# Second self-attention: where sums, inverses, scaling and output products stand in the slots

## Chip, cores and metric

The kernel runs on one core of one Trainium2 chip. The metric is the time of one execution on the device in microseconds (us), lower is better; the median of several runs is compared.

## What is computed

Two transformer blocks run one after the other over x of shape (8, 512, 256): eight batch rows ("batches" here) of 512 tokens. All arithmetic is float32. The change is in the first attention of the second block, self-attention with 16 heads of width 64 and rotary positions:

```
attn_in = adaln(x, cond)
q, k, v = attn_in @ wq, attn_in @ wk, attn_in @ wv      # (512, 1024) each, 16 heads of 64
q, k = rope(q), rope(k)
a = softmax(q @ k.T * 64 ** -0.5)                       # per head, 512 x 512
x = (a @ v) @ wo + bo + x                               # heads joined, 1024 -> 256
```

Softmax is computed without subtracting a maximum: the exponentials are multiplied with v first, and the result is divided by the exponentials' sums afterwards.

## The kernel before

The kernel runs through phases: the first block (to about 835 us), this self-attention (about 835 to 1820 us), and cross-attention with the feed-forward part (to the end). In every phase the order of the work on TensorE (PE), VectorE (DVE), ScalarE (ACT) and GpSimd (POOL) is the order in which the Python code issues it: the block is under a manual schedule, and nothing is reordered. Each engine runs its own instructions in that order and waits for data and buffers. DMAs of this phase are issued from SyncE's queue (SP), also in order.

**Blocks and groups.** A batch's 16 heads are four groups `g` of four heads; keys are four tiles `kt` of 128. A block is one pair (g, kt): `score(g, kt)` makes 8 products into two tiles ps_S (each two PSUM banks), which ACT turns with two exponentials (L1020) into two tiles p (six buffers in all). `value(g, kt)` multiplies p with v into the banks ps_O and ps_D, over the four kt; after the last one ACT copies them into two tiles oT (L1043).

**Sums of a group.** At kt 0 POOL adds the p tiles of kt 0 and 1 into two tiles sm (L1035). At kt 2 DVE adds those of kt 2 and 3 (four operations L1039). Then `sums(g)` adds over the 128 partitions by products with ones (`ones32`, 32 columns wide) into a bank ps_X; ACT copies it to den (L1055), and two DMAs bring it through DRAM into a tile rec. `inverse(g)` is a reciprocal (L1067) and two small reductions (L153) on DVE, a DMA to DRAM (rec_d) and four DMAs that spread it over partitions into two tiles rb. `scaled(g)` multiplies both oT with rb on POOL (L1085). When all eight oT of a batch are scaled, `out_tiles(0)` and `out_tiles(1)` multiply them with w_so, 32 products each into one ps_X bank, and DVE adds the bank to x (L464).

**Preparing q, k, v.** `values(half, ts)` computes two token tiles of v into two ps_X banks, which ACT copies (L989). `queries(g)` and `keys(g)` make two banks each; DVE multiplies each bank with cosines (L999) and sines (L1000) into four tiles t, and POOL combines them (L1002, L1003). There are two ps_X banks, used in turn by values, queries, keys, sums, outputs and the transposes of `turn`.

**Slots.** A slot m holds two blocks: scores of block 2m+1, then the jobs of that slot, then scores of block 2m+2, then values of blocks 2m and 2m+1, then what `after` holds. A batch b has eight slots, `base = 8 b`; this text counts them 0 to 7. Even slots compute values of kt 0 and 1, odd ones of kt 2 and 3. The jobs of batches in the middle, in order (next: of the batch after; prev: of the batch before):

| slot | jobs between the two scores | after the values |
|---|---|---|
| 0 | values, sums(3, prev), keys(1), layer-norm statistics (next) | inverse(3, prev) |
| 1 | values, queries(2), scaled(3, prev) | |
| 2 | output 0 (prev), sums(0), keys(2), statistics (next) | layer-norm rows (next), inverse(0) |
| 3 | output 1 (prev), queries(3), row addition to x (POOL, L448), scaled(0) | |
| 4 | keys(3), sums(1), turn (next): 8 transposes (L427) | inverse(1) |
| 5 | queries(0, next), scaled(1) | |
| 6 | values (next), sums(2), keys(0, next) | inverse(2) |
| 7 | values (next), queries(1, next), scaled(2) | |

The place of sums comes from `mid`, which is put behind the slot's first job. In the first batch, slot 4 has a memset as its first job, so sums stand ahead of the keys there.

Of the kernel before, what the change touches and what calls it, by code (L numbers as in the profile page):

```python
# [17 lines left out]
B, N, D, H, T, CD, FF = 8, 512, 256, 16, 64, 192, 1024  # L18
# [67 lines left out]
def fast_path(ctx: ExitStack, tc: tile.TileContext, a: dict, out: bass.AP):  # L86
# [878 lines left out]
    with tc.tile_pool(name="ph4", bufs=2) as wk:  # L965
        NG = H // 4
        kb, vb = kv_first()
        first_rows = []
        steps, mid, after = {}, {}, {}

        def last(slot, fn):
            steps.setdefault(slot, []).append(fn)
# [152 lines left out]
        for b, (score, value, sums, inverse, scaled, out_tiles, _) in enumerate(todo):  # L1125
            base = 2 * NG * b
            for g in range(NG):
                if b == B - 1 and g == NG - 1:
                    break
                n = base + 2 * g + 2  # L1130
                mid[n] = lambda g=g, f=sums: f(g)
                after.setdefault(n, []).append(lambda g=g, f=inverse: f(g))
                last(n + 1, lambda g=g, f=scaled: f(g))
            if b < B - 1:
                for qp in range(2):
                    steps[base + 2 * NG + 2 + qp].insert(0, lambda qp=qp, f=out_tiles: f(qp))

        def slots():
            n = B * NG * NT
# [1029 lines left out]
@with_exitstack  # L2169
def tile_kernel(ctx: ExitStack, tc: tile.TileContext, a: dict, out: bass.AP):  # L2170
    nc = tc.nc
    with ExitStack() as fast:
        good = fast_path(fast, tc, a, out)
        flag = nc.values_load(good[0:1, 0:1], min_val=0, max_val=1,
                              skip_runtime_bounds_check_because="it is made by a comparison")
    with tc.If(flag == 0):
        with ExitStack() as general:
            general_path(general, tc, a, out)
# [86 lines left out]
```

## Time and profile before

| | us |
|---|---|
| median of 3 runs (lowest, highest) | 2419.1 (2417.03, 2423.43) |
| the profiled execution's own time | 2413.91 |
| its span, first to last instruction | 2411.8 |
| one batch in the middle of this self-attention | 122.5 |

| engine | busy us | share of the span |
|---|---|---|
| PE (products) | 2379.0 | 99% |
| DVE | 1139.5 | 47% |
| POOL | 966.5 | 40% |
| ACT | 889.2 | 37% |

The granted TensorE clock is 0.998 of full speed. A line of the timeline gives the start (us from the span's start), the time to the end of the last merged instruction, the engine, the line of the kernel, what is written and read, how many instructions are merged and, in brackets, how long the engine was idle before them and what released it. Every product in float32 shows as two instructions. Products are pipelined, so their ends overlap the next start: differences of starts are the better measure.

### The profile page before, as it was taken

How to read it: one execution, taken by the hardware profiler on the slowest of the kernel's cores; microseconds unless marked ns; L12 is line 12 of the kernel's file. 1: busy time of each engine (PE TensorE's matmuls, PEld its weight loads, DVE VectorE, ACT ScalarE, POOL GpSimd, SP SyncE). 2: the span in 40 equal slices, each digit the busy share in tenths (PEclk: the TensorE clock that was granted, in tenths of full speed). 3: DMA queues.
4: the chain of work that ended last, by engine and by line, in shares of the span. 5: the costliest groups of instructions: out<-in, count | busy, mean ns of one | idle time of the engine just before them, and what ended most of it. 6: DMA issues, size and time to landing. Idle time of an engine off the chain costs nothing.

```text
span 2411.8 us, 28553 instructions
## 1 busy us (share of the span) xinstructions
PE 2379.0 (99%) x10964; PEld 1158.8 (48%) x10964; DVE 1139.5 (47%) x2115; ACT 889.2 (37%) x1118; POOL 966.5 (40%) x588
## 2 busy tenths in 40 slices
PE   9999999999999999999999999999999999999998
PEld 4333544544545633434343444444445556567665
DVE  4564534434345344555454555545445656651110
ACT  4665545545442134333333333333342212221221
POOL 4563323323201046555555554646453445441110
PEclk9999999999999999999999999999999999999999
DMA  5130000000002001000101010100023212210000
GB/s 184 33 107 11 16 15 13 16 14 6 12 11 92 0 1 32 14 24 10 28 10 28 10 28 10 28 10 26 30 67 95 77 58 68 64 56 31 18 22 20
DMA packets 84897, 84.07 MB, mean 35 GB/s; under 512 B 42656, under 2 KB 59792, under 8 KB 84752
## 3 DMA queue, kind: packets, MB, share of 16 engines
q1 hardware_dynamic: 83208, 78.99, 11.0%
q8 instruction: 88, 1.44, 0.2%
q0 software_dynamic: 640, 2.10, 0.2%
q10 hardware_dynamic: 904, 1.07, 0.2%
q14 instruction: 57, 0.47, 0.1%
HBM read 72.09 MB, written 10.04 MB: 34 GB/s over the span
## 4 chain that ended last, share of the span: by engine, by line
PE 87%; DVE 4%; POOL 3%; issue 3%; DMA 1%; ACT 1%; SPq 1%; POOLq 0%; DVEq 0%; ACTq 0%
PE ps_X L116 36%; PE ps_S L116 22%; PE ps_D L116 13%; PE ps_O L116 13%; PE ps_X L427 1%; DMA rb<-rec 1%; DVE t L843 1%; POOL x L448 1%; DVE sm L1039 1%; POOL p L1277 1%; ACT p L590 0%; PE ps_X L610 0%; POOL var L561 0%; DVE t L1000 0%; SPq L1270 0%
## 5 line engine op out<-in xcount | busy, mean ns | idle before, releaser
L116 PE MATMUL ps_S<-q,k 32*128 32x512 f32 (+1 forms) x3072 | 425.6, 623 | 5.5 <-ACT p L590 3.4
L1020 ACT ACTIVATE p<-ps_S 128x1024 f32<-128x1024 f32 x256 | 250.8, 1022 | 459.7 <-PE ps_S L116 450.3
L590 ACT ACTIVATE p<-ps_S 128x1024 f32<-128x1024 f32 x256 | 248.3, 1022 | 171.6 <-PE ps_S L116 170.3
L116 PEld LDWEIGHTS ps_S<-q,k 32*128 32x128 f32 (+1 forms) x3072 | 148.7, 183 | 244.8 <-issue 155.5
L1039 DVE TENSOR_TENSOR sm<-sm,p 128x1024 f32<-128x1024 f32 x128 | 252.1, 2028 | 0.1
L999 DVE TENSOR_TENSOR t<-ps_X,rope_c 128x512 f32<-128x512 f32 x126 | 87.0, 690 | 341.0 <-PE ps_X L116 341.0
L1002 POOL TENSOR_TENSOR q<-t 128x512 f32<-128x512 f32 x32 | 65.5, 2047 | 294.3 <-DVE t L1000 294.3
L182 POOL TENSOR_TENSOR rstd<-rstd,mhalf 128x4 f32<-128x4 f32 x49 | 51.2, 1044 | 293.6 <-DVE rstd L181 292.6
L844 POOL TENSOR_TENSOR q<-t,t 128x512 f32<-128x512 f32 x72 | 94.9, 1319 | 172.6 <-DVE t L843 171.6
L116 PE MATMUL ps_X<-hT,w 128*128 128x512 f32 x328 | 151.0, 597 | 0.5 <-DVE t L780 0.5
L1035 POOL TENSOR_TENSOR sm<-p 128x1024 f32<-128x1024 f32 x64 | 149.7, 2364 | 1.9 <-ACT p L1020 1.9
L1085 POOL TENSOR_TENSOR oT<-oT,rb 128x512 f32<-128x512 f32 x63 | 128.9, 2065 | 19.6 <-DMA rb<-rec_d 19.6
L116 PE MATMUL ps_O<-p,v 128*64 128x512 f32 x512 | 134.9, 605 | 0.0
L116 PE MATMUL ps_D<-p,v 128*64 128x512 f32 x512 | 131.6, 592 | 0.0
L116 PE MATMUL ps_O<-p,h 128*32 128x512 f32 x1024 | 129.5, 609 | 0.6 <-ACT p L590 0.6
L621 POOL TENSOR_TENSOR attn<-attn,gate 128x256 f32<-128x256 f32 x32 | 23.3, 727 | 250.7 <-DVE attn L619 250.7
L116 PE MATMUL ps_X<-w_sa_wv,hT 128*128 128x512 f32 x256 | 118.0, 604 | 0.0
L1002 POOL TENSOR_TENSOR k<-t 128x512 f32<-128x512 f32 x32 | 40.7, 1272 | 192.8 <-DVE t L1000 192.8
L116 PE MATMUL ps_X<-hT,w_sa_wq 128*128 128x512 f32 x256 | 115.9, 595 | 0.0
L116 PE MATMUL ps_X<-w_sa_wo,oT 128*128 128x256 f32 x512 | 114.5, 382 | 0.1
L116 PE MATMUL ps_X<-hT,w_sa_wk 128*128 128x512 f32 x248 | 114.6, 605 | 0.0
L116 PE MATMUL ps_S<-hT,w_ff_w 128*128 128x512 f32 x256 | 111.3, 593 | 0.0
(286 smaller groups left out, 3663.6 us busy)
## 6 DMA issues: line engine op xcount, KB each, us to landing
rb<-rec SPq DMA_DIRECT2D x128, 128.0 KB
rb<-rec_d SPq DMA_DIRECT2D x124, 128.0 KB
rb<-rec SPq DMA_DIRECT2D x16, 256.0 KB
out_dram<-x SPq DMA_DIRECT2D x15, 256.0 KB
x<-in_x_dram SPq DMA_DIRECT2D x7, 512.0 KB
gate<-modd SPq DMA_DIRECT2D x24, 128.0 KB
k_d<-q POOLq DMA_DIRECT2D x8, 256.0 KB, 2.4
v_d<-v SPq DMA_DIRECT2D x8, 256.0 KB
```

What stands on the lines that cost most here:

```text
L116: nc.tensor.matmul(o, lhsT, rhs, start=start, stop=stop)
L182: nc.gpsimd.tensor_tensor(r[:, :n], r[:, :n], mhalf[:, :n], ALU.pow)
L427: nc.tensor.transpose(ps[:, t * P : (t + 1) * P], z[:, t, k * P : (k + 1) * P], ident)
L448: nc.gpsimd.tensor_tensor(xs[b], xs[b], r[:, None, :].to_broadcast([P, NT, D]), ALU.add)
L590: nc.scalar.activation(pr[u], pss[u], AF.Exp, scale=HD0 ** -0.5)
L844: nc.gpsimd.tensor_tensor(dst, t1, t2, ALU.add)
L999: nc.vector.tensor_tensor(c, ps, rope_c, ALU.mult)
L1002: nc.gpsimd.tensor_tensor(r[0], ec, os, ALU.subtract)
L1020: nc.scalar.activation(pr, pss[u], AF.Exp, scale=HD1 ** -0.5)
L1035: nc.gpsimd.tensor_tensor(sm, s["p", g, 0, u], s["p", g, 1, u], ALU.add)
L1039: nc.vector.tensor_tensor(s["sm", g, u], s["sm", g, u], s["p", g, t, u], ALU.add)
L1085: eng.tensor_tensor(o, o, s["rb", g, u], ALU.mult)
```

## The change

For the groups of every batch but the last, sums move from between the slot's jobs to the head of what follows the slot's values; the inverse moves from the end of that slot to the end of the next slot's jobs; scaling moves one slot further. Both output products of a batch stand together at the head of slot 3 of the next batch, instead of one in slot 2 and one in slot 3. The groups of the last batch keep their places.

```diff
                 n = base + 2 * g + 2
-                mid[n] = lambda g=g, f=sums: f(g)
-                after.setdefault(n, []).append(lambda g=g, f=inverse: f(g))
-                last(n + 1, lambda g=g, f=scaled: f(g))
+                if b == B - 1:
+                    mid[n] = lambda g=g, f=sums: f(g)
+                    after.setdefault(n, []).append(lambda g=g, f=inverse: f(g))
+                else:
+                    after.setdefault(n, []).insert(0, lambda g=g, f=sums: f(g))
+                    last(n + 1, lambda g=g, f=inverse: f(g))
+                last(n + 1 + (b < B - 1), lambda g=g, f=scaled: f(g))
             if b < B - 1:
-                for qp in range(2):
-                    steps[base + 2 * NG + 2 + qp].insert(0, lambda qp=qp, f=out_tiles: f(qp))
+                steps[base + 2 * NG + 3][0:0] = [lambda qp=qp, f=out_tiles: f(qp) for qp in range(2)]
```

The slots of a batch in the middle after the change:

| slot | jobs between the two scores | after the values |
|---|---|---|
| 0 | values, keys(1), statistics (next), scaled(2, prev) | sums(3, prev) |
| 1 | values, queries(2), inverse(3, prev) | |
| 2 | keys(2), statistics (next), scaled(3, prev) | sums(0), layer-norm rows (next) |
| 3 | output 0, output 1 (prev), queries(3), row addition to x, inverse(0) | |
| 4 | keys(3), turn (next), scaled(0) | sums(1) |
| 5 | queries(0, next), inverse(1) | |
| 6 | values (next), keys(0, next), scaled(1) | sums(2) |
| 7 | values (next), queries(1, next), inverse(2) | |

## Prediction

> **What bounds the kernel now.** I read the page first, then PE's timeline over one batch of the second self-attention (122.5 us a batch), then the timelines of POOL, ACT and DVE beside it, and the waits.
>
> ```profile
> PE 2379.0 (99%) x10964; PEld 1158.8 (48%) x10964; DVE 1139.5 (47%) x2115; ACT 889.2 (37%) x1118; POOL 966.5 (40%) x588
> ```
>
> PE is the bound: 99% busy. In one batch of this phase (1181.40 to 1303.90) it is busy 122.00 of 122.50 us, so the change is worth what it does to PE's own sequence, and what new waits it puts before PE. PE's timeline, slots 0 and 1, then slot 4 (start, us, ...):
>
> ```profile
> 1211.58 2.00 PE L116 MATMUL ps_S<-q,k 32*128 32x512 f32 x16
> 1213.51 3.70 PE L116 MATMUL ps_X<-w_sa_wv,hT 128*128 128x512 f32 x8
> 1217.14 1.06 PE L116 MATMUL ps_X<-sm,ones 128*32 128x512 f32 x8
> 1218.14 3.70 PE L116 MATMUL ps_X<-hT,w_sa_wk 128*128 128x512 f32 x8
> 1221.77 2.00 PE L116 MATMUL ps_S<-q,k 32*128 32x512 f32 x16
> ...
> 1227.28 2.00 PE L116 MATMUL ps_S<-q,k 32*128 32x512 f32 x16
> 1229.21 3.70 PE L116 MATMUL ps_X<-w_sa_wv,hT 128*128 128x512 f32 x8
> 1232.75 3.60 PE L116 MATMUL ps_X<-hT,w_sa_wq 128*128 128x512 f32 x8
> ...
> 1280.87 3.70 PE L116 MATMUL ps_X<-hT,w_sa_wk 128*128 128x512 f32 x8
> 1284.94 1.06 PE L116 MATMUL ps_X<-sm,ones 128*32 128x512 f32 x8 [0.37 <-DVE t L1000]
> 1286.14 1.23 PE L427 MATMUL ps_X<-ident,z 128*128 128x128 f32 x8
> 1287.30 2.00 PE L116 MATMUL ps_S<-q,k 32*128 32x512 f32 x16
> ```
>
> The reader is to see starts, not durations: start to start, values, sums, keys take 8.26 (1213.51 to 1221.77), values and queries without sums 7.07 (1229.21 to 1236.28). So sums in the middle cost 1.20. The only wait is slot 4's 0.37. Sums that stand behind values already exist at the end of the phase (PE's timeline again):
>
> ```profile
> 1791.75 1.03 PE L116 MATMUL ps_D<-p,v 128*64 128x512 f32 x4
> 1792.70 1.07 PE L116 MATMUL ps_X<-sm,ones 128*32 128x512 f32 x8
> 1793.70 2.00 PE L116 MATMUL ps_S<-q,k 32*128 32x512 f32 x16
> ```
>
> Values to sums 0.95, sums to scores 1.00; elsewhere values to scores take 0.96. So sums there cost 0.99.
>
> POOL of slot 0, and a scaling pair with nothing in its way; ACT of slot 1; and one line of ACT's waits over seven batches (us, times, longest):
>
> ```profile
> 1223.38 1.27 POOL L1002 TENSOR_TENSOR k<-t 128x512 f32<-128x512 f32 x1 [6.94 <-DVE t L1000]
> 1225.84 4.67 POOL L1035 TENSOR_TENSOR sm<-p 128x1024 f32<-128x1024 f32 x2
> ...
> 1787.58 2.56 POOL L1085 TENSOR_TENSOR oT<-oT,rb 128x512 f32<-128x512 f32 x2 [4.30 <-DMA rb<-rec_d]
> ```
> ```profile
> 1229.38 2.19 ACT L1020 ACTIVATE p<-ps_S 128x1024 f32<-128x1024 f32 x2 [3.63 <-PE ps_S L116]
> 1231.46 0.58 ACT L989 COPY v<-ps_X 128x512 f32<-128x512 f32 x1
> ```
> ```profile
> ACT p L1020 <- POOL sm L1035: 7.3, 7, 1.2
> ```
>
> POOL's two first additions end at 1230.51, and slot 1's second exponential can only start then: its p tile (6 buffers, two a block) was last read by them. The pair takes 2.19 where others take 1.94. Then comes the copy of the values' bank, done at 1232.04; the queries' first product reuses that bank (two X banks) at 1232.75. So a chain POOL, ACT, PE has 0.7 us to spare.
>
> **What the Trainium skill says.** "TensorEngine Tiling (Array Packing)", Key Properties: a change of tiling mode drains the array. The trace agrees: sums (32 columns) between full-array products cost 1.20, but only 0.86 start to start when they follow products that are themselves 32 columns wide. "SBUF — State Buffer", Who interferes with whom: a DVE operation with two SBUF inputs and a POOL operation reading SBUF exclude one another. It agrees: DVE's sums additions (L1039) take 1.21 alone and 2.29 beside POOL, a scaling 1.27 and 2.25. "PSUM — Partial Sum Buffer", Engine vs sequencer instructions: the queues of ACT, DVE and POOL are strictly first in, first out; the bank copy stuck behind a waiting exponential is that.
>
> **The change part by part** (a slot is counted 0 to 7 in its batch).
>
> *Sums, slots 0 and 6.* Middle to end: -1.20 + 0.99 = -0.21 each. Seven of each: **-2.9**. The price behind the values is bounded by 0.86 and 1.20; I take the direct row.
>
> *Slots 2 and 3.* Before, start to start, one output, sums and keys take 11.73, one output and queries 10.55: 22.28. After: keys 3.63; two outputs and queries 10.55 + 6.92 (an output's 32 products) = 17.47; sums 0.99: 22.09. -0.2 for seven batches, nothing for the first, which has no output: **-1.4**. Joining the outputs costs nothing in itself; what covers it: the first output's bank is wanted back 7 us later, and DVE's addition into x takes 0.69; ACT's exponentials for the next block have 17 us.
>
> *Slot 4.* Keys take both X banks, and the turn's transposes now take them straight after. DVE frees them late: it stands behind the four additions L1039, which begin after the queries of slot 3 and end at 1283.61. After the change two things move there. The inverse (0.24 + 0.24 us) comes before the additions, so POOL's first query operation gets the port first (0.8 later, of which a part returns); and scaling no longer alternates with the last addition. Played through with the pairs measured (2.22 for an addition beside a 512-wide POOL operation, 3.29 beside the row addition L448, 1.13 alone): 1276.2 + 1.1 + 2.2 + 3.3 + 1.1 = 1283.9 to 1284.1, 0.3 to 0.5 later. The second bank, free at 1286.09 before, is then free at 1286.5, and four transposes later (0.57) scores begin at about 1287.1 instead of 1287.30: -0.2. Sums at the end add 0.99: +0.8. Six batches: +4.8. In the first batch sums stand ahead of keys and wait 1.82, the second transpose 0.87; there 9.45 becomes 6.2, and +0.99: -2.2. Sum: **+2.6**.
>
> *Scaling goes from odd to even slots.* On POOL it now stands between the keys' rotation and the first additions L1035. In slot 0, DVE is idle by then apart from statistics with one input, so the pair costs 2.47 (two start-to-start steps of 1.23). Against the start of slot 1, the additions end later by 2.47 - 1.20 (keys come sooner without sums) + 0.21 (slot 1 starts sooner) = 1.48. The exponential, then the bank's copy, follow: copy done 6.24 after the slot's start instead of 4.76; queries want the bank at 5.47. The wait is 6.24 + 0.05 - 5.47 = 0.82 (0.05 from the end of a release to the product, as in slot 4). Behind the waiting exponential stand both copies of v, then the next block's exponentials, which PE's values need only 6 us later; behind PE's wait stands everything, so the slot is longer by it. Slots 6 and 7 have the same jobs. Seven slots 1 and seven slots 7: 14 x 0.82 = **+11.5**. Slot 3 has the wait on p too, but two outputs ahead of any bank that ACT frees; slot 5 computes queries alone, no bank copy, and the additions end 2.7 after its start, before they are wanted (3.2): nothing there. Upper bound: if scaling alternated with DVE, 2.25 each, 2.0 more per wait; lower bound: no wait.
>
> *Inverse one slot on.* DVE's wait on the DMA goes (46.3 us in ten waits, all in DVE's idle time): worth nothing. The SP queue keeps its order, den_d, rec, rec_d, four rb; from inverse to rb landed some 6 us (1265.95, the last rb issued by 1270.1 and about 2 to land, my estimate), and scaling comes 10 us or more after that inverse. In the first batch the loads of kb now stand ahead of one rec_d on SP; the same slack covers them. Without it POOL's scaling, and behind it the additions that slots 1 and 7 wait for, would be late by as much. The same DMAs, instructions and bytes are issued.
>
> Sum: -2.9 - 1.4 + 2.6 + 11.5 = **+9.8 us**. Against the profiled execution's 2413.9 that is 2423.7. That execution is 5.2 below the median of the runs; on the median, 2419.1, it gives **2428.9**.
>
> **Rivals.**
> 1. *The p wait does not bind* (chance 0.22). Point of decision: the additions end less than 0.66 us later against the slot's start. For it: POOL stands idle 6.94 before slot 0's keys, and anything that brings keys sooner takes from the 1.48. Against: the buffers are already waited for (2.19 for 1.94). Then +9.8 - 11.5 = -1.7, no difference; if slot 4's DVE were early too (-0.21 instead of +0.8 in six batches), -7.8, faster.
> 2. *The additions or scaling meet DVE on the port* (0.06): 2.0 more in 14 waits, +28, so +38. Against: keys' rotation beside statistics takes 1.27 to 1.29, no more than alone.
> 3. *The pair of outputs stalls the queries of slot 3* (0.1): DVE's layer-norm pieces, each 2.43 beside POOL's additions and now started later, run into the slot; rstd is ready some 10.4 us into slot 2, then scaling, additions and pieces take turns for 8.5 us; with slot 2 now 12.2 long they end about 7 us into slot 3, and the first output ends 9 us in. If they ran 4 us longer, the queries of seven batches would wait up to 1 to 2 us: +17 to +24.
> 4. The order is written out by hand, so the change cannot be undone by a planner.
>
> **How the numbers follow.** Forecast 0.62, its own range +5 to +15 (sums 0.86 to 1.05, wait 0.6 to 1.1, slot 4 ±0.4 each). With part of rivals 1 and 3: 2418 to 2440. About 0.3%, 7.3 us, is what a measurement of this kernel can tell from no change. Slower by more: most of the forecast (0.52) and rivals 2 and 3: 0.68. Faster: the end of rival 1: 0.07. Within: 0.25.
>
> **What would show it.** Values to sums to scores 0.95 and 1.00 in every even slot; no sums between full-array products but in the last batch. A wait of about 0.8 before the queries of slots 1 and 7, released by ACT's copy v (L989), and a total of ACT p on POOL sm far above 7.3. In slot 4 a wait of the transposes on DVE t (L1000). No such wait in slots 3 and 5. Wrong if slots 1 and 7 begin their queries 3.5 after their values: then the second rival's opposite, the first, holds; or if outputs in slot 3 show a gap.

## Result and the profile after

The changed kernel takes 2433.5 us (median of 6 runs, 2428.1 to 2438.3) against 2421.1 (median of 6, 2415.6 to 2423.4). The ratio is 1.0058, 95% interval 1.0040 to 1.0076: slower by 0.58%, some 12 to 14 us. The forecast was +9.8, to 2428.9, within 2418 to 2440. The profiled execution took 2428.13; its span, first to last instruction, is 2426.3.

PE's timeline of the changed kernel, slots 0 and 1, then slot 4, the counterpart of the lines in the prediction (start us, us, engine, line, operation, count, idle before and what ended it):

```profile
1215.18 2.00 PE L116 MATMUL ps_S<-q,k 32*128 32x512 f32 x16
1217.11 3.70 PE L116 MATMUL ps_X<-w_sa_wv,hT 128*128 128x512 f32 x8
1220.64 3.60 PE L116 MATMUL ps_X<-hT,w_sa_wk 128*128 128x512 f32 x8
1224.17 2.00 PE L116 MATMUL ps_S<-q,k 32*128 32x512 f32 x16
...
1228.72 1.03 PE L116 MATMUL ps_D<-p,v 128*64 128x512 f32 x4
1229.68 1.06 PE L116 MATMUL ps_X<-sm,ones 128*32 128x512 f32 x8
1230.68 2.00 PE L116 MATMUL ps_S<-q,k 32*128 32x512 f32 x16
1232.61 3.70 PE L116 MATMUL ps_X<-w_sa_wv,hT 128*128 128x512 f32 x8
1236.95 3.70 PE L116 MATMUL ps_X<-hT,w_sa_wq 128*128 128x512 f32 x8 [0.65 <-ACT v L989]
1240.59 2.00 PE L116 MATMUL ps_S<-q,k 32*128 32x512 f32 x16
...
1284.98 3.70 PE L116 MATMUL ps_X<-hT,w_sa_wk 128*128 128x512 f32 x8
1289.35 0.66 PE L427 MATMUL ps_X<-ident,z 128*128 128x128 f32 x4 [0.66 <-DVE t L1000]
1290.87 0.66 PE L427 MATMUL ps_X<-ident,z 128*128 128x128 f32 x4 [0.87 <-ACT hT L428]
```

Three things are to be seen. From the last values to sums it is 0.96, from sums to scores 1.00, start to start. In slot 1 the queries begin 4.34 after the values, not 3.54, and what they waited for is ACT's copy of v. In slot 4 the eight transposes come as two groups of four, each group filling one bank; sums used to stand between them and the keys, and now both groups wait.

The chain of waits behind slot 1, in POOL's timeline and then ACT's:

```profile
1225.78 1.28 POOL L1002 TENSOR_TENSOR k<-t 128x512 f32<-128x512 f32 x1 [10.64 <-DVE t L1000]
1227.00 1.29 POOL L1003 TENSOR_TENSOR k<-t 128x512 f32<-128x512 f32 x1
1228.23 2.53 POOL L1085 TENSOR_TENSOR oT<-oT,rb 128x512 f32<-128x512 f32 x2
1230.70 4.67 POOL L1035 TENSOR_TENSOR sm<-p 128x1024 f32<-128x1024 f32 x2
```
```profile
1233.09 1.02 ACT L1020 ACTIVATE p<-ps_S 128x1024 f32<-128x1024 f32 x1 [1.69 <-POOL sm L1035]
1235.40 1.02 ACT L1020 ACTIVATE p<-ps_S 128x1024 f32<-128x1024 f32 x1 [1.28 <-POOL sm L1035]
1236.32 1.07 ACT L989 COPY v<-ps_X 128x512 f32<-128x512 f32 x2
```

Scaling (2.47 from its start to that of the additions) now runs ahead of the additions, which end at 1235.37; the second exponential starts at 1235.40, the copies stand behind it, and the queries' first product starts at 1236.95, 0.05 after the first of the two copies ends (1236.90). That p's six buffers are what is scarce is read from the name of ACT's wait; more buffers were not tried. PE's waits over the phase, then one line of ACT's between 880 and 1690 us (total us, times, longest):

```profile
PE ps_X L116 <- ACT v L989: 9.2, 14, 0.9
PE ps_X L427 <- ACT hT L428: 6.1, 7, 0.9
PE ps_X L427 <- DVE t L1000: 4.7, 7, 0.7
```
```profile
ACT p L1020 <- POOL sm L1035: 60.9, 37, 2.8
```

These are fourteen waits of the queries, as counted in the prediction, and ACT's waits on POOL's additions are up from 7.3 to 60.9 us. Not all of the 60.9 reaches PE: 25.0 of it lies in slot 3, as the first experiment shows.

Spans of single executions differ mostly by stretches in which PE's granted clock is half ("half clock" below), most of them in the first 200 us, before this phase: the first scores of slot 0 start between 855 and 867 us in the nine profiles. So the experiments are read by slot, start of scores to start of scores. One batch in the middle, us (slots 2 and 3 together; 5 is 11.07 in all):

| kernel | 0 | 1 | 2+3 | 4 | 6 | 7 | batch |
|---|---|---|---|---|---|---|---|
| before | 15.70 | 14.51 | 37.15 | 13.87 | 15.70 | 14.51 | 122.51 |
| changed | 15.50 | 15.42 | 36.96 | 14.92 | 15.50 | 15.41 | 124.78 |
| scale_behind | 15.50 | 14.51 | 36.96 | 14.92 | 15.50 | 14.51 | 122.97 |
| scale_late | 15.70 | 16.41 | 36.96 | 13.87 | 15.70 | 16.40 | 126.11 |
| outs_pair | 15.70 | 14.51 | 36.96 | 13.87 | 15.70 | 14.51 | 122.31 |
| sums4_mid | 15.50 | 15.42 | 36.96 | 14.22 | 15.50 | 15.41 | 124.08 |
| inv_head | 15.50 | 15.42 | 36.96 | 13.91 | 15.50 | 15.41 | 123.77 |
| scale_dve | 15.50 | 14.51 | 36.96 | 14.92 | 15.50 | 14.51 | 122.97 |
| best | 15.50 | 14.51 | 36.96 | 13.62 | 15.50 | 14.51 | 121.67 |

Rows repeat from batch to batch within 0.03, except where a half-clock stretch falls into a slot, in a few slots of the seventh batch (up to 0.3 more), in the first batch, which has no outputs before it, and in the last, which ends otherwise.

### The profile page after: what moved, and what is told of

Same layout as the page of the kernel before. It is cut to its first block, busy times and chain, and to the rows that moved or that the text cites. A ratio compares the mean times of both kernels' runs of the same rounds, so it can differ in the third digit from the quotient of the medians.

```text
span 2426.3 us, 28542 instructions
## 1 busy us (share of the span) xinstructions
PE 2379.2 (98%) x10964; PEld 1160.0 (48%) x10964; DVE 1122.0 (46%) x2115; ACT 888.5 (37%) x1118; POOL 897.4 (37%) x588
## 4 chain that ended last, share of the span: by engine, by line
PE 80%; POOL 6%; DVE 5%; issue 4%; ACT 2%; DMA 1%; SPq 0%; POOLq 0%; DVEq 0%; ACTq 0%
PE ps_X L116 33%; PE ps_S L116 20%; PE ps_D L116 12%; PE ps_O L116 12%; POOL sm L1035 3%; POOL oT L1085 1%; PE ps_X L427 1%; DMA rb<-rec 1%; POOL k L1003 1%; DVE t L843 1%; DVE sm L1039 1%; DVE t L1000 1%; ACT p L1020 1%; DVE t L999 1%; POOL p L1280 1%
## 5 line engine op out<-in xcount | busy, mean ns | idle before, releaser
L1039 DVE TENSOR_TENSOR sm<-sm,p 128x1024 f32<-128x1024 f32 x128 | 225.9, 1822 | 0.1
L1002 POOL TENSOR_TENSOR q<-t 128x512 f32<-128x512 f32 x32 | 42.3, 1323 | 314.8 <-DVE rec L1067 227.0
L561 POOL TENSOR_TENSOR var<-var,mhalf 128x32 f32<-128x32 f32 (+1 forms) x17 | 87.4, 5140 | 55.1 <-DVE var L555 55.0
```

What stands on the lines that cost most here:

```text
L561: nc.gpsimd.tensor_tensor(var, var, half, ALU.pow)
L1002: nc.gpsimd.tensor_tensor(r[0], ec, os, ALU.subtract)
L1039: nc.vector.tensor_tensor(s["sm", g, u], s["sm", g, u], s["p", g, t, u], ALU.add)
```

## Experiments

**scale_behind: is it scaling's place in POOL's queue?** From the changed kernel:

```diff
-                last(n + 1 + (b < B - 1), lambda g=g, f=scaled: f(g))
+                if b < B - 1 and g in (1, 2):
+                    after.setdefault(n + 2, []).append(lambda g=g, f=scaled: f(g))
+                else:
+                    last(n + 1 + (b < B - 1), lambda g=g, f=scaled: f(g))
```

> The changed kernel with one thing moved: scaling of groups 1 and 2 (slots 6 and 0) stands behind POOL's first additions L1035 of that slot instead of ahead of them. Theory A (scaling ahead of the additions keeps p tiles, ACT's copy of v and so the queries' bank waiting): slots 1 and 7 go from 15.41 back to 14.51 us, no wait of the queries on ACT v L989, total about 12.6 below the changed kernel's span, so about 2412 to 2414. Theory B (the loss comes from where sums stand): slots 1 and 7 stay at 15.4, span 2425 or so. Slot 4 stays at 14.9 in both.

Slots 1 and 7 are 14.51 again in every batch. PE's waits no longer hold a line of ACT v L989, and ACT's line is

```profile
ACT p L1020 <- POOL sm L1035: 25.0, 13, 2.8
```

of which none reaches PE: they lie in slot 3, where two outputs follow. POOL's timeline shows the exchanged order, additions first:

```profile
1232.19 4.67 POOL L1035 TENSOR_TENSOR sm<-p 128x1024 f32<-128x1024 f32 x2
1236.82 2.51 POOL L1085 TENSOR_TENSOR oT<-oT,rb 128x512 f32<-128x512 f32 x2
```

Timed: 2421.4 against 2420.1, ratio 1.0001 (0.9987 to 1.0015). Its profiled span, 2419.4, missed the 2412 to 2414 expected: the half-clock stretches ahead of the phase made it start late (slot 0 at 864.1 us, against 855.3 before). The slots and the ratio decide: theory A holds, and this one order accounts for nearly the whole net loss. What is left in the seven batches is 0.6: slot 4's loss less the sums' gains.

**scale_late: late scaling without the moved sums.** From the kernel before:

```diff
-                last(n + 1, lambda g=g, f=scaled: f(g))
+                last(n + 1 + (b < B - 1), lambda g=g, f=scaled: f(g))
 ...
-                for qp in range(2):
-                    steps[base + 2 * NG + 2 + qp].insert(0, lambda qp=qp, f=out_tiles: f(qp))
+                steps[base + 2 * NG + 3][0:0] = [lambda qp=qp, f=out_tiles: f(qp) for qp in range(2)]
```

> The kernel before with scaling one slot later and both outputs in slot 3 (which late scaling needs); sums and inverses where they were. Theory A: POOL's first additions end 2.47 later in slots 0 and 6, with 0.66 to spare: slots 1 and 7 go from 14.51 to about 16.3, 14 times 1.8 = +25, span about 2436, more than the whole change cost, as keys come 1.2 later behind sums in the middle. Theory B (sums are the loss): span 2410 to 2412.

Slots 1 and 7: +1.90 and +1.89, and PE's wait is named the same (872 to 1690 us):

```profile
PE ps_X L116 <- ACT v L989: 19.9, 12, 1.9
```

Late scaling without the moved sums and inverses costs twice what it costs with them. That they return 1.0 of the 1.9 fits the keys, which come 1.2 sooner when no sums stand ahead of them. The moved sums do not cause the wait; they soften it. The one execution took 2449.9; its span, 2447.8, is 12 above the 2436 expected: the phase began 8.2 later than before, and one slot 1, with a stretch at half clock in it, took 2.0 more.

**outs_pair: the two outputs together.** From the kernel before, only the second half of the last diff.

> The kernel before with both outputs together at the head of slot 3, nothing else moved. Theories A and B: slots 2 and 3 together 36.9 to 37.2 against 37.15, span 2410 to 2412. Theory C (two outputs in one slot stall the queries or the scores): slot 3 longer by 1 to 2 us in seven batches, span 2419 to 2426.

Slots 2 and 3 take 36.96 instead of 37.15. No wait is added; the 0.19 fits that sums of group 0, whose place is behind the slot's first job, then stand behind slot 2's keys and no longer between an output and keys. Theory C falls. The one execution took 2416.1; its span, 2413.9, missed the 2410 to 2412 expected, as the phase began 3.6 later than before.

**sums4_mid: cover for slot 4.** From the changed kernel:

```diff
-                    after.setdefault(n, []).insert(0, lambda g=g, f=sums: f(g))
+                    if g == 1 and b:
+                        mid[n] = lambda g=g, f=sums: f(g)
+                    else:
+                        after.setdefault(n, []).insert(0, lambda g=g, f=sums: f(g))
```

> The changed kernel with the sums of group 1 back between keys and the turn in slot 4 (batches 1 to 6), inverse and scaling late as changed. Theory A: only slot 4 changes, from 14.92 to 14.0 to 14.2 (the sums cover DVE's lateness again, which stays 0.3 more than before), 6 times 0.8 = -5, slots 1 and 7 stay at 15.4; span about 2420. Theory B: slots 1 and 7 fall too.

Slot 4 falls from 14.92 to 14.22, slots 1 and 7 stay at 15.4. PE waits before sums instead of before the first transposes, and both groups then follow unbroken:

```profile
1297.17 1.06 PE L116 MATMUL ps_X<-sm,ones 128*32 128x512 f32 x8 [0.68 <-DVE t L1000]
1298.37 1.27 PE L427 MATMUL ps_X<-ident,z 128*128 128x128 f32 x8
```

The span missed the 2420 or so expected (2430.5), again by what lies ahead of the phase: its first slot 0 starts 9.2 later than in the changed kernel's profile.

**inv_head: why 14.22 and not 13.87.** From sums4_mid:

```diff
-                    last(n + 1, lambda g=g, f=inverse: f(g))
+                    if g == 0:
+                        steps.setdefault(n + 1, []).insert(0, lambda g=g, f=inverse: f(g))
+                    else:
+                        last(n + 1, lambda g=g, f=inverse: f(g))
```

> The kernel with the sums of group 1 back in the middle of slot 4, and the inverse of group 0 at the head of slot 3 instead of behind the queries. Theory A (the inverse ahead of DVE's additions lets POOL's query rotation take the port first, and DVE ends 0.35 later): slot 4 falls from 14.22 to 13.87, the value of the kernel before; all other slots unchanged (15.5, 15.4, 12.07, 24.89). Rival (the 0.35 is the missing scaling on POOL, or keys' place): slot 4 stays at 14.2.

Slot 4 takes 13.91. DVE's additions follow the sines at once, as before the change, and so get their turn before POOL's query rotation, whose first operation takes 2.10 again (2.10 before, 1.27 in the changed kernel). PE's wait is back to 0.4 (2.2 in six). The inverse's place cost 0.3 of slot 4; the last 0.04 is open.

**scale_dve: the same place, another engine.** From the changed kernel, groups 1 and 2:

```diff
+                if b < B - 1 and g in (1, 2):
+                    last(n + 2, lambda g=g, f=scaled: f(g, [nc.vector] * 2))
 ...
```

> The changed kernel with scaling of groups 1 and 2 in its changed place, ahead of the first additions, but on DVE instead of POOL. Theory A (POOL's delay is what counts, not the place of scaling in the slot): POOL is held up by the port alone, at most about 1.3, against 2.47; less 1.0 for keys that come sooner this stays below the 0.66 to spare, and slots 1 and 7 are 14.5 to 14.8 instead of 15.41; total 10 to 12 less than the changed kernel. Rival (late scaling itself costs, through oT or rb): slots 1 and 7 stay at 15.4.

Both slots take 14.51. The same multiplications at the same place cost PE nothing in these slots when DVE makes them. POOL is still held up, beside DVE's scaling (k L1003 took 1.29 in the changed kernel, the pair of additions 4.67):

```profile
1225.98 1.73 POOL L1003 TENSOR_TENSOR k<-t 128x512 f32<-128x512 f32 x1
1227.66 5.12 POOL L1035 TENSOR_TENSOR sm<-p 128x1024 f32<-128x1024 f32 x2
```

That is 0.4 twice in place of 2.5, inside what there is to spare. The one execution took 2416.8.

**best: what the change offers without its two losses.** From the changed kernel, the edits of sums4_mid, scale_behind and inv_head together, and the row addition to x moved from slot 3 to slot 5:

```diff
-                last(base - 5, lambda: add_row(b, row("sabo")))
                 last(base - 4, turn)
                 last(base - 3, lambda: queries(0))
+                last(base - 3, lambda: add_row(b, row("sabo")))
```

> The changed kernel with four edits: scaling of groups 1 and 2 behind POOL's first additions; sums of group 1 between keys and turn (batches 1 to 6); the inverse of group 0 at the head of slot 3; the row addition L448 moved from slot 3 to slot 5 behind the queries. Theory A: slots 1 and 7 14.51, slots 0 and 6 15.5, slots 2 and 3 together 36.95; slot 4 without DVE's lateness 13.3 to 13.5 (before 13.87, changed 14.92), in the first batch about 14.3 to 14.9. Against the kernel before -1.4 -1.2 -1.4 in the three, 6 times -0.45 and -2 to -2.6 in slot 4: about -8 to -9 us, ratio 0.9965. If the row addition in slot 5 delays slot 6 (keys' banks), slot 6 is longer than 15.5.

2413.2 (median of 22) against 2419.6 (median of 27), ratio 0.9972 (0.9962 to 0.9981): faster than the kernel before by 0.28%, and so than the changed one. Slot 4 is 13.62, a little above the 13.3 to 13.5 expected: the first transposes still wait 0.46 for DVE to free a bank of the keys. In the first batch it is 14.03, below the 14.3 to 14.9 expected. Slot 6 stays at 15.50, so the row addition in slot 5 delays nothing. By slots the seven batches take 8.0 less than before. What the row addition's move alone is worth was not run.

## Why the prediction was right, point by point

By slots, over all eight batches and without one half-clock stretch, the change adds 13.2 us; forecast 9.8. The direction, the place of the loss and the count of waits were forecast; two terms were sized too small, both on the same side, so the result within the range does not come from errors that cancel. Term by term:

| term | forecast | measured |
|---|---|---|
| sums to the end, slots 0 and 6 | -2.9 | -2.8 (14 x -0.20) |
| slots 2 and 3 | -1.4 | -1.3 (7 x -0.19) |
| slot 4, six batches and the first | +4.8, -2.2 | +6.3, -2.0 |
| queries' wait, slots 1 and 7 | +11.5 | +13.0 |

*Sums.* The two steps read at the phase's end, 0.95 and 1.00, held to 0.01 at every place. The reading that would have misled was the cheaper row, 0.86, measured where sums follow products as narrow as themselves.

*Queries' wait.* The mechanism, its place and count were right. The delay itself was 0.80 (4.34 against 3.54; forecast 0.82), but the queries' block then takes 3.63 to 3.64 instead of the 3.53 that it takes directly behind the values. The prediction added the delay alone; the 0.1 that it left out is +1.4 over fourteen slots. In one slot of the seventh batch the wait was 0.27 longer: POOL began the rotation of that batch's slot 0 keys 0.29 later than in other batches, though DVE was not late. Why is open.

*Slot 4.* The first group's wait was forecast well (DVE frees the bank at 1289.29, 4.31 after the keys' start, against 4.02 before: 0.29 late, forecast 0.3 to 0.5), and inv_head shows the inverse's place to be nearly all of its cause. The step that failed is the second group of transposes. The prediction gave it the keys' second bank, which DVE frees at 1290.49; it started at 1290.87, 0.05 after ACT's copy of the first group:

```profile
1289.82 0.67 DVE L1000 TENSOR_TENSOR t<-ps_X,rope_s 128x512 f32<-128x512 f32 x1
1290.04 0.78 ACT L428 ACTIVATE hT<-ps_X,b,a 128x512 f32<-128x512 f32 x1 [3.02 <-PE ps_X L427]
```

In the built program both groups have the same bank: unlike what was said ahead of the prediction, the two ps_X banks are not always used in turn. That is the missing 0.25 a batch (1.05 measured, 0.8 forecast). The kernel before shows the same wait where transposes follow keys directly, in its first batch, where both groups have one bank too:

```profile
917.71 0.60 PE L427 MATMUL ps_X<-ident,z 128*128 128x128 f32 x4
919.18 0.66 PE L427 MATMUL ps_X<-ident,z 128*128 128x128 f32 x4 [0.87 <-ACT hT L428]
```

The prediction quoted this 0.87, but counted no such wait after the change. In the six batches where sums stand between keys and transposes (before, sums4_mid and best), the built programs give the two groups different banks, and the second group does not wait. What was not run is keys directly ahead of transposes with a bank for each group.

*Half clock.* In this profile slot 4 of the fourth batch takes 16.56: the scores after the two waits take 3.63 instead of 2.00. The trace's clock record shows 3.4 us at 0.5 from 1291.7 on. The Trainium skill ("TensorE: Matmul & The Clock Gate", Part 1) describes a gate that follows PE's recent activity in windows of 3.4 us; the length agrees. In the 3.4 us ahead of it PE was idle for 0.66 and 0.87. Of the other profiles only scale_late's has such a stretch inside this phase, from 1630.6 on, directly behind the longest wait of its queries (1.92). That the new waits make such stretches likelier is a guess: all the other waits of these sizes passed without one.

*Rivals.* The first (the p wait does not bind) was wrong for the change but is just what scale_behind and scale_dve make true; their first seven batches take 0.6 more than before in all. Scaling did not meet DVE in the changed kernel (2.53 for the pair), nor did the outputs stall the queries: in slot 3 queries follow outputs at once. The inverse's wait on the DMA (46.3 us in ten waits before, 21.7 in four now) was worth nothing to PE, as said, and from an inverse to its scaling, some 6 us in the prediction's estimate, a direct row at the end of the phase before gives 5.4 (1782.18 to 1787.58), inside the slack; what its move did cost came from DVE's order, not from the DMA.

## What to carry to other kernels

When a step moves to a slot where its engine "has time", look at what is queued behind it there and at which buffer those operations free: here 2.5 us of POOL ahead of the last readers of a six-buffer tile reached PE through two queues, with 0.66 us to spare. Put work that nobody waits for behind the last reader of a scarce buffer. A short product that separates two users of the same bank is a cover as well as a cost: moving it away paid in slots 0 and 6, where the bank was free, and lost in slot 4, where it was not.

## What the runs showed of the hardware that was not expected

A block of full-array products takes 3.53 start to start directly behind another such block, and 3.63 to 3.64 after a wait, so a delay of 0.8 costs 0.9 here. A wait is not needed for it: in the kernel before, keys behind sums take 3.63 too (1218.14 to 1221.77). With scaling no longer beside them, DVE's four sums additions take 6.65 instead of 7.86 in slots 1, 5 and 7, and POOL's busy time falls from 966.5 to 897.4: two engines that do not bind spent less time on the same work while the kernel became slower.
